# A router's top two found inside the attention stage, two groups at a time, in place of its logits

## The chip, the cores and the metric

One Trainium2 chip, one core. The metric is the device time of one execution in microseconds (us), the median of three runs. Kernel and reference work in float32. TensorE is called PE, VectorE DVE, ScalarE ACT, GpSimd POOL; SP is the engine whose queue issues most DMAs.

## What is computed

The input x has 4 sequences of 2048 tokens with 256 features. Three residual blocks follow each other:

```python
x = x + 0.5 * ffn(layernorm(x))
x = x + attn(layernorm(x))
x = x + 0.5 * ffn(layernorm(x))
```

`ffn` is a mixture of 8 experts. The part that matters here is its router:

```python
logits = xf @ router_w.T                 # 8192 tokens x 8 experts
probs = softmax(logits)
topw, topi = top_k(probs, 2)
topw = topw / (topw.sum(-1) + 1e-6)
# each expert keeps its 1280 tokens of highest weight (ties by token number)
# and adds weight * (silu(x@wg) * (x@wu)) @ wd to them
```

`attn` is a gated delta-rule recurrence over time with 8 heads of 32 features (projections, a chain over time, a gated norm and an output projection), and a small MLP with silu behind it.

## The kernel before

Five stages follow each other on the one core: the first layer norm with the first router logits (`first_norm`), `route` and `experts` for the first mixture, `attention`, and `route` and `experts` for the second. In the profile they take about 0 to 117, 117 to 207, 207 to 1080, 1080 to 2592 and 2592 to 3569 us.

`attention` cuts time into 64 chunks of 32 steps. The 128 partitions hold 4 sequences by 32 steps; four chunks are a group, so there are 16 groups, g = 0 to 15. A group passes five generators: `stage_load`, `stage_proj`, `stage_prep` (decays, and the triangular inverse on DVE in lines 870 to 891), `stage_chain` (the recurrence) and `stage_out` (lines 973 to 1044). `weave` (line 1048) runs the generators of neighbouring groups by turns. Each `yield` gives the PE time, the wait and the DVE work of the step just emitted, and `weave` picks the next step from these numbers and from due times with a period of 78 us. PE keeps exactly the order that `weave` emits. The other engines are ordered by the framework's scheduler when the program is built, by program order and by priorities (`urgent()` and `first()` raise them). On the chip each engine takes its instructions strictly in that order and waits on semaphores.

What `stage_out` does, by line: 976 to 978 scale the sums of squares `sx` and run a Newton reciprocal root (`newton`, lines 643 to 648) into `rx`; 988 makes `hh` on ACT from it, which PE transposes (658); 997 to 1018 are the MLP; 1023 to 1027 the layer norm's statistics; 1031 makes `xn`; 1036 transposes it; 1040 multiplies by the router's weights into `pl`; 1041 copies the 8 logits of each of the 128 tokens of a chunk into the tile `logits2` (128 partitions, 64 chunks by 8 experts); 1043 stores `xn`. Other instructions that the prediction names: `qa` and `gg` (lines 758 to 771, a series for softplus in `stage_prep`, DVE), `gm` (777, POOL, four instructions per group, made from `gg`), `pd` (798, PE, from `gm`), `Z` (923) and `OS` (930), DVE transposes of the recurrence that PE waits for, `O` (938), and the POOL products of lines 816 to 867 and 980.

`top2` (line 169) does the router's softmax and picks the two experts. It has 24 DVE instructions and one ACT Exp, nearly all in one chain: each takes what the one before it made. It is called four times in `first_norm`, for 16 chunks each, and once behind `attention`, for all 64 chunks (line 1155). Its result W lies expert by expert, `[P, E, NCH]`, while the logits and its inner tiles lie chunk by chunk, `[P, NCH, E]`. `route` then copies W to ACT (316), stores it to DRAM and reads it back in another layout (324, 326), and starts a search for each expert's threshold (336 and on); `find` (291) and `place` (463) are constants that it loads on the SP queue.

Of the kernel before, what the change touches and what calls it, by code (L numbers as in the profile page):

```python
# [9 lines left out]
F32 = mybir.dt.float32  # L10
# [3 lines left out]
ALU = mybir.AluOpType  # L14
AX = mybir.AxisListType
# [3 lines left out]
P = 128  # L19
B = 4  # L20
C = 32
GC = 4
# [3 lines left out]
E = 8  # L26
# [61 lines left out]
def bc(ap, axes, shape):  # L88

    for a in axes:  # L90
        ap = ap.unsqueeze(a)
    return ap.to_broadcast(list(shape))
# [3 lines left out]
def macaron_kernel(  # L96
# [5 lines left out]
    nc = tc.nc  # L102
    T = x.shape[1]
    NCH = T // C
# [6 lines left out]
    xf, outf = (a.rearrange("b t d -> (b t) d") for a in (x, out))  # L111
# [13 lines left out]
    with tc.tile_pool(name="cst_b", bufs=1) as bp:  # L125
        brief = bp.tile([P, _W - _KEPT], F32, name="cst_b")
# [34 lines left out]
    def store_group(rows, xt, g):  # L161
        for b in range(B):
            r0 = b * T + g * GC * C
            nc.sync.dma_start(
                out=rows[r0 : r0 + GC * C, :].rearrange("(c t) d -> t c d", t=C),
                in_=xt[b * C : (b + 1) * C, :, :],
            )

    def top2(pool, logits, W):

        n = logits.shape[1]
        TE = [P, n, E]

        def t(shape, name):
            return pool.tile(shape, F32, tag=f"t2_{name}", name=name)

        mx, pr, sm = t([P, n], "mx"), t(TE, "pr"), t([P, n], "sm")
        nc.vector.tensor_reduce(mx, logits, AX.X, ALU.max)
        nc.vector.tensor_tensor(pr, logits, bc(mx, [2], TE), ALU.subtract)
        nc.scalar.activation(pr, pr, AF.Exp)  # L180
        nc.vector.tensor_reduce(sm, pr, AX.X, ALU.add)
        nc.vector.reciprocal(sm, sm)
        nc.vector.tensor_tensor(pr, pr, bc(sm, [2], TE), ALU.mult)

        rev = bc(K["rev8"], [1], TE)
        oh, mk = [], []
        for k in range(2):
            mxk, f, fm, ohk = t([P, n], f"mx{k}"), t(TE, "first"), t([P, n], "fm"), t(TE, f"oh{k}")
            nc.vector.tensor_reduce(mxk, pr, AX.X, ALU.max)
            nc.vector.tensor_tensor(f, pr, bc(mxk, [2], TE), ALU.is_equal)  # L190
            nc.vector.tensor_tensor(f, f, rev, ALU.mult)
            nc.vector.tensor_reduce(fm, f, AX.X, ALU.max)
            nc.vector.tensor_tensor(ohk, rev, bc(fm, [2], TE), ALU.is_equal)
            if k == 0:
                nc.vector.scalar_tensor_tensor(pr, ohk, -2.0, pr, ALU.mult, ALU.add)
            oh.append(ohk)
            mk.append(mxk)
        den = t([P, n], "den")
        nc.vector.tensor_tensor(den, mk[0], mk[1], ALU.add)
        nc.vector.tensor_scalar(den, den, 1e-6, None, ALU.add)  # L200
        nc.vector.reciprocal(den, den)
        for k in range(2):
            nc.vector.scalar_tensor_tensor(mk[k], mk[k], 0.5, den, ALU.mult, ALU.mult)
            nc.vector.tensor_tensor(oh[k], oh[k], bc(mk[k], [2], TE), ALU.mult)
        nc.vector.tensor_tensor(W.rearrange("p e c -> p c e"), oh[0], oh[1], ALU.add)

    def first_norm(brief, W, xn_d):

        MC = 8
        xc, nc_ = (a.rearrange("(p c) d -> p c d", p=P) for a in (xf, xn_d))
        logits = brief.tile([P, NCH, E], F32, name="logits")
        with tc.tile_pool(name="in", bufs=3) as ip, tc.tile_pool(name="in_t", bufs=3, space=PSUM) as tps, tc.tile_pool(
            name="in_l", bufs=2, space=PSUM
        ) as lps:
            some = [MC // 2] * 2
            c0 = 0
            for IC in some + [MC] * ((NCH - 2 * MC) // MC) + some:
                xt = ip.tile([P, MC, D], F32, name="xt_in")[:, :IC, :]  # L220
                nc.sync.dma_start(out=xt, in_=xc[:, c0 : c0 + IC, :])
                st = ip.tile([P, MC, 6], F32, name="in_st")
                mv = ip.tile([P, MC, 2], F32, name="in_mv")[:, :IC, :]
                for c in range(IC):
                    nc.vector.bn_stats(st[:, c, :], xt[:, c, :])
                    nc.vector.bn_aggr(mv[:, c, :], st[:, c, :])
                ve = ip.tile([P, MC], F32, name="in_ve")[:, :IC]
                nc.vector.tensor_scalar(ve, mv[:, :, 1], LN_EPS, None, ALU.add)
                r = ip.tile([P, MC], F32, name="in_r")[:, :IC]
                rsqrt(ip, r, ve, IC, "in")  # L230
                nm = ip.tile([P, MC], F32, name="in_nm")[:, :IC]
                nc.vector.scalar_tensor_tensor(nm, mv[:, :, 0], -1.0, r, ALU.mult, ALU.mult)
                xn = ip.tile([P, MC, D], F32, name="in_xn")[:, :IC, :]
                for c in range(IC):
                    if c % 2:
                        nc.scalar.activation(
                            xn[:, c, :], xt[:, c, :], AF.Identity, scale=r[:, c : c + 1], bias=nm[:, c : c + 1]
                        )
                    else:
                        nc.vector.tensor_scalar(  # L240
                            xn[:, c, :], xt[:, c, :], mv[:, c, 0:1], r[:, c : c + 1], ALU.subtract, ALU.mult
                        )
                nc.sync.dma_start(out=nc_[:, c0 : c0 + IC, :], in_=xn)
                pl = lps.tile([P, MC, E], F32, name="pl_in")[:, :IC, :]
                for c in range(0, IC, 2):
                    tp = tps.tile([P, 2, 2, P], F32, name="tp_in")
                    for i in range(2):
                        for k in range(2):
                            nc.tensor.transpose(tp[:, i, k, :], xn[:, c + i, k * P : (k + 1) * P], ident)
                    xnT = ip.tile([P, 2, 2, P], F32, name="in_xnT")  # L250
                    nc.scalar.copy(xnT, tp)
                    for i in range(2):
                        for k in range(2):
                            nc.tensor.matmul(  # L254
                                pl[:, c + i, :], xnT[:, i, k, :], rw[:, k, :], start=(k == 0), stop=(k == 1)
                            )
                nc.scalar.copy(logits[:, c0 : c0 + IC, :], pl)
                c0 += IC
                if c0 % (2 * MC) == 0:
                    cs = slice(c0 - 2 * MC, c0)  # L260
                    top2(ip, logits[:, cs, :], W[:, :, cs])

    behind = tc.keep_in_program_order

# [309 lines left out]
                    if t0 == 0 and e + 1 < E:  # L574
                        find(e + 1)

    def attention(x1_d, logits, xn_d, x2_d):
        GH = GC * H
        CH = [P, GC, H]
        CHI = [P, GC, H, C]  # L580
# [1 line left out]
        with ExitStack() as st:  # L582
# [3 lines left out]
            wp, p1, p2, p3, p4 = pool("w", 1), pool("1", 1), pool("2", 2), pool("3", 3), pool("4", 4)  # L586
# [386 lines left out]
            def stage_out(g):  # L973
# [9 lines left out]
                for c0 in range(0, GC, 2):  # L983
                    hT2 = p2.tile([P, 2, 2 * P], F32, tag="hT2", name="hT2")
                    for i in range(2):
                        c = c0 + i
# [18 lines left out]
                    for i in range(2):  # L1005
                        c = c0 + i
# [23 lines left out]
                for c in range(GC):  # L1030
                    nc.scalar.activation(
                        xn[:, c, :], xt[:, c, :], AF.Identity, scale=r3[:, c : c + 1], bias=nm3[:, c : c + 1]
                    )
                    yield 0, 0.6
                    xnT = p3.tile([P, 2, P], F32, tag="hT", name="xnT")
                    transposed(xn[:, c, :], xnT)
                    yield 0.25, 0.7
                    pl = tpp.tile([P, E], F32, tag="tp", name="pl")
                    for k in range(2):
                        nc.tensor.matmul(pl, xnT[:, k, :], rw[:, k, :], start=(k == 0), stop=(k == 1))  # L1040
                    nc.scalar.copy(logits[:, g * GC + c, :], pl)
                    yield 0.4, 0.3
                store_group(xn_d, xn, g)
                del live[g]

            plans = {}
# [88 lines left out]
    xn2 = dram.tile([N, D], F32, name="xn2")  # L1135
# [9 lines left out]
                experts(1, wp, ready, place16, *found, xn1, x1_d)  # L1145


    logits2 = keep.tile([P, NCH, E], F32, name="logits2")
    attention(x1_d, logits2, xn2, outf)


    with tc.tile_pool(name="brief2", bufs=1) as brief:
        W = brief.tile([P, E, NCH], F32, name="W2")
        with tc.tile_pool(name="top2", bufs=1) as pool:
            top2(pool, logits2, W)
        with tc.tile_pool(name="ex_w2", bufs=2) as wp, tc.tile_pool(name="place2", bufs=1) as rp:
            ready, place16 = [], places(rp, 2)
            found = route(brief, 2, W, wp, ready, xn2)
            with tc.manual_schedule(engines={mybir.EngineType.PE}):
                experts(2, wp, ready, place16, *found, xn2, outf)  # L1160

# [28 lines left out]
```

## Time and profile before

| what | value |
|---|---|
| runs | 3569.07, 3577.85, 3581.4 us (median 3577.85) |
| profiled execution | 3570.8 us, its span 3569.0 us |
| granted PE clock, mean | 0.96 |
| PE, matmul busy | 3149.7 us, 88% of the span |
| DVE busy | 1665.6 us, 47% |
| ACT busy | 966.8 us, 27% |
| POOL busy | 739.1 us, 21% |
| table loads on ACT (1283 ns each) | 50 |
| last logits copied (line 1041) | begins at 2592.19 us |
| W2 written (line 205) | ends at 2607.41 us |

A line of a time line reads: start, duration, engine, line of the kernel, operation, output from inputs, shapes, count, and in brackets the idle time of that engine just before and what ended it. A busy PE is not PE at its peak, since matmuls are pipelined. The granted clock is 1.0 or 0.5 in each interval; a mean under 1 says for what share of the time PE ran at half rate.

### The profile page before, as it was taken

To read this page: it belongs to the slowest core of one execution; us is meant where nothing else is said; L and a number is where in the kernel's file an instruction comes from. 1 tells how busy PE (TensorE), PEld (TensorE's weight loads), DVE (VectorE), ACT (ScalarE), POOL (GpSimd) and SP (SyncE) were. 2 spreads that over 40 slices of the span, in tenths; PEclk is the share of its full clock that TensorE was granted. 3 is DMA by queue.
4 is the path that set the end of the run, shared out by engine and by line. 5 is a ranking of instruction groups with operands and counts; after the bars stand their busy time and mean duration, and the time that the engine had idled before them with its cause. 6 is when DMAs were issued, how large, how long until landed. Compare 5 with 4: busy or idle time off the path is not lost.

```text
span 3569.0 us, 74202 instructions
## 1 busy us (share of the span) xinstructions
PE 3149.7 (88%) x31911; PEld 2162.5 (61%) x31911; DVE 1665.6 (47%) x4844; ACT 966.8 (27%) x2222; POOL 739.1 (21%) x794
## 2 busy tenths in 40 slices
PE   7279999999995588999999999899817999999998
PEld 6246666666662366666666666667714666666666
DVE  6751222221116747778777777665284122222111
ACT  3212211112213233343443434333221122111121
POOL 0031332222211111112112122111003123222121
PEclk9999999999997799999999999999858999999999
DMA  4512222222112000010110000000021222122211
GB/s 171 198 24 58 64 51 40 60 52 59 30 15 70 2 20 3 20 26 19 26 27 20 20 20 20 14 14 15 19 87 30 54 61 65 27 60 59 54 27 15
DMA packets 94791, 153.10 MB, mean 43 GB/s; under 512 B 13368, under 2 KB 77760, under 8 KB 92800
## 3 DMA queue, kind: packets, MB, share of 16 engines
q1 hardware_dynamic: 63648, 106.15, 9.5%
q0 software_dynamic: 30816, 42.23, 7.4%
q8 instruction: 250, 4.10, 0.5%
q14 instruction: 77, 0.63, 0.1%
HBM read 101.67 MB, written 55.05 MB: 44 GB/s over the span
## 4 chain that ended last, share of the span: by engine, by line
PE 71%; DVE 21%; ACT 3%; issue 2%; DMA 2%; POOL 1%; SPq 0%; POOLq 0%; DVEq 0%; ACTq 0%
PE pg L551 15%; PE po L564 15%; PE pu L553 15%; DVE tm L875 4%; DVE X L879 4%; PE pp L718 3%; PE py L1009 3%; PE pc L635 3%; PE pgk L635 2%; PE pl_in L254 1%; PE ppo L965 1%; DVE over L357 1%; PE tp L658 1%; PE tpx L525 1%; PE pd L798 1%
## 5 line engine op out<-in xcount | busy, mean ns | idle before, releaser
L556 DVE TENSOR_TENSOR hT<-sg,pu 128x512 f32<-128x512 f32 (+1 forms) x384 | 229.3, 597 | 1136.7 <-PE pu L553 1135.5
L551 PE MATMUL pg<-xT,wg_e 128*128 128x512 f32 (+1 forms) x1536 | 617.4, 524 | 0.9 <-ACT xT L526 0.9
L553 PE MATMUL pu<-xT,wu_e 128*128 128x512 f32 (+1 forms) x1536 | 613.4, 522 | 0.0
L564 PE MATMUL po<-wd_e,hT 128*128 128x256 f32 x2560 | 560.4, 379 | 0.0
L564 PEld LDWEIGHTS po<-wd_e,hT 128*128 128x128 f32 x2560 | 485.3, 190 | 73.1 <-issue 8.6
L553 PEld LDWEIGHTS pu<-xT,wu_e 128*128 128x128 f32 x1536 | 292.3, 190 | 259.5 <-issue 243.6
L551 PEld LDWEIGHTS pg<-xT,wg_e 128*128 128x128 f32 x1536 | 280.8, 191 | 204.3 <-issue 191.5
L555 ACT ACTIVATE sg<-pg 128x512 f32<-128x512 f32 (+1 forms) x384 | 201.9, 526 | 688.4 <-PE pg L551 685.5
L1009 PE MATMUL py<-wpj,mT 128*128 128x256 f32 x1024 | 264.2, 393 | 15.6 <-DVE xt L1016 8.7
L519 POOL DMA_INDIRECT xg<-xn,idx x160 | 198.7, 1242 | 366.4 <-PE tpx L525 188.3
L718 PE MATMUL pp<-wk,hT 128*128 128x512 f32 x512 | 269.5, 622 | 5.6 <-ACT hT L660 5.4
L570 POOL DMA_INDIRECT x_d<-eo,idx x80 | 131.0, 1638 | 543.5 <-ACT eo L569 378.2
L570 POOL DMA_INDIRECT out_dram<-eo,idx x80 | 128.9, 1611 | 543.5 <-ACT eo L569 374.1
L1009 PEld LDWEIGHTS py<-wpj,mT 128*128 128x128 f32 x1024 | 185.2, 191 | 74.1 <-DVE xt L1016 17.7
L491 DVE TENSOR_TENSOR oa<-aM,iota 128x2048 bf16<-128x2048 bf16 x64 | 145.5, 2283 | 161.6 <-PE pi L503 161.6
L569 ACT ACTIVATE eo<-po,ws 128x256 f32<-128x256 f32 x160 | 75.8, 473 | 522.2 <-PE po L564 522.2
L980 POOL TENSOR_TENSOR xt<-xt,x 128x256 f32<-128x256 f32 x64 | 48.4, 757 | 720.6 <-DVE x L967 373.3
L875 DVE TENSOR_TENSOR tm<-X 128x30 f32<-128x30 f32 (+14 forms) x480 | 156.2, 325 | 11.1
L879 DVE TENSOR_TENSOR X<-X,tm 128x30 f32<-128x30 f32 (+14 forms) x480 | 155.5, 324 | 10.9
L526 ACT COPY xT<-tpx 128x256 f32<-128x256 f32 x160 | 59.6, 372 | 255.8 <-PE tpx L525 255.8
L718 PEld LDWEIGHTS pp<-wk,hT 128*128 128x128 f32 x512 | 89.7, 195 | 41.8 <-issue 22.8
L635 PE MATMUL pc<-WQD,OS 32*32 32x96 f32 x4032 | 108.2, 246 | 1.5 <-issue 1.5
(744 smaller groups left out, 4006.6 us busy)
## 6 DMA issues: line engine op xcount, KB each, us to landing
wg_e<-in_L_ffn_wg_dram SPq DMA_DIRECT2D x16, 1024.0 KB, 5.2
wu_e<-in_L_ffn_wu_dram SPq DMA_DIRECT2D x16, 1024.0 KB, 6.9
wd_e<-in_L_ffn_wd_dram SPq DMA_DIRECT2D x16, 1024.0 KB, 5.7
xt<-x_d SPq DMA_DIRECT2D x64, 128.0 KB, 3.0
out_dram<-xt SPq DMA_DIRECT2D x64, 128.0 KB, 2.3
xn<-xn SPq DMA_DIRECT2D x64, 128.0 KB, 2.3
xt_in<-in_L_attn_x_dram SPq DMA_DIRECT2D x6, 1024.0 KB, 7.0
xn<-in_xn SPq DMA_DIRECT2D x6, 1024.0 KB, 4.8
```

The costliest lines, as they stand in the source:

```text
L519: nc.gpsimd.indirect_dma_start(out=xg, out_offset=None, in_=xn_d[:], in_offset=bass.IndirectOffsetOnAxis(ap=idx[:, t : t + 1], axis=0),)
L551: nc.tensor.matmul(pg[:, :n], wg_e[:, k, fs], xT[:, k, cols], start=(k == 0), stop=(k == 1))
L553: nc.tensor.matmul(pu[:, :n], wu_e[:, k, fs], xT[:, k, cols], start=(k == 0), stop=(k == 1))
L555: nc.scalar.activation(sg[:, :n], pg[:, :n], AF.Silu)
L556: nc.vector.tensor_tensor(hT[:, f, :n], sg[:, :n], pu[:, :n], ALU.mult)
L564: nc.tensor.matmul(po, hT[:, f, (t - t0) * P : (t - t0 + 1) * P], wd_e[:, f, :], start=(f == 0), stop=(f == FF // P - 1),)
L570: nc.gpsimd.indirect_dma_start(out=acc[:], out_offset=bass.IndirectOffsetOnAxis(ap=idx[:, t : t + 1], axis=0), in_=eo, in_offset=None, com ...
L635: nc.tensor.matmul(out[q], lhsT[q], rhs[q], start=first, stop=True, skip_group_check=True)
L718: nc.tensor.matmul(pp, hT[:, k, :], wk[:, k, j * 2 * D : (j + 1) * 2 * D], start=(k == 0), stop=(k == 1),)
L875: nc.vector.tensor_tensor(tmv, Xm[:, j + 1 :, j : j + 1].to_broadcast([P, n, j]), Xm[:, j : j + 1, :j].to_broadcast([P, n, j]), ALU.mult,)
L879: nc.vector.tensor_tensor(Xm[:, j + 1 :, :j], Xm[:, j + 1 :, :j], tmv, ALU.add)
L1009: nc.tensor.matmul(py, mT[:, f, i * P : (i + 1) * P], wpj[:, f, :], start=(f == 0), stop=(f == FF // P - 1),)
```

## The change

`top2` gets W alone and works in it: the copies out of PSUM put the logits straight into W, and softmax and the two picks run in W through a view that swaps experts and chunks. The separate tile `pr` and the logits tiles go. In `attention` the second router's `top2` is called at the end of `stage_out` of every odd group, for the 8 chunks of that group and the one before, with its small tiles in a pool of `attention` with one buffer. The single call for 64 chunks behind `attention` goes. No `yield` follows the new call, so `weave` counts nothing for it.

```diff
-    def top2(pool, logits, W):
-        n = logits.shape[1]
+    def top2(pool, W):
+        n = W.shape[2]
+        pr = W.rearrange("p e c -> p c e")
...
-        nc.vector.tensor_reduce(mx, logits, AX.X, ALU.max)
-        nc.vector.tensor_tensor(pr, logits, bc(mx, [2], TE), ALU.subtract)
+        nc.vector.tensor_reduce(mx, pr, AX.X, ALU.max)
+        nc.vector.tensor_tensor(pr, pr, bc(mx, [2], TE), ALU.subtract)
...
-        nc.vector.tensor_tensor(W.rearrange("p e c -> p c e"), oh[0], oh[1], ALU.add)
+        nc.vector.tensor_tensor(pr, oh[0], oh[1], ALU.add)
...
     # first_norm
-                nc.scalar.copy(logits[:, c0 : c0 + IC, :], pl)
+                nc.scalar.copy(W[:, :, c0 : c0 + IC].rearrange("p e c -> p c e"), pl)
...
-                    top2(ip, logits[:, cs, :], W[:, :, cs])
+                    top2(ip, W[:, :, cs])
...
     # stage_out of attention
-                    nc.scalar.copy(logits[:, g * GC + c, :], pl)
+                    nc.scalar.copy(W[:, :, g * GC + c], pl)
                     yield 0.4, 0.3
                 store_group(xn_d, xn, g)
+                if g % 2:
+                    top2(p1, W[:, :, (g - 1) * GC : (g + 1) * GC])
                 del live[g]
...
-    logits2 = keep.tile([P, NCH, E], F32, name="logits2")
-    attention(x1_d, logits2, xn2, outf)
+    W2 = keep.tile([P, E, NCH], F32, name="W2")
+    attention(x1_d, W2, xn2, outf)
...
-        W = brief.tile([P, E, NCH], F32, name="W2")
-        with tc.tile_pool(name="top2", bufs=1) as pool:
-            top2(pool, logits2, W)
```

More of the change, by code (lines that the diff above doesn't have):

```diff
@@ L175, in t @@
             return pool.tile(shape, F32, tag=f"t2_{name}", name=name)
-        mx, pr, sm = t([P, n], "mx"), t(TE, "pr"), t([P, n], "sm")
-        nc.vector.tensor_reduce(mx, logits, AX.X, ALU.max)
-        nc.vector.tensor_tensor(pr, logits, bc(mx, [2], TE), ALU.subtract)
+        mx, sm = t([P, n], "mx"), t([P, n], "sm")
+        nc.vector.tensor_reduce(mx, pr, AX.X, ALU.max)
+        nc.vector.tensor_tensor(pr, pr, bc(mx, [2], TE), ALU.subtract)
         nc.scalar.activation(pr, pr, AF.Exp)
@@ L212, in first_norm @@
         xc, nc_ = (a.rearrange("(p c) d -> p c d", p=P) for a in (xf, xn_d))
-        logits = brief.tile([P, NCH, E], F32, name="logits")
         with tc.tile_pool(name="in", bufs=3) as ip, tc.tile_pool(name="in_t", bufs=3, space=PSUM) as tps, tc.tile_pool(
@@ L575, in experts, with attention @@
                         find(e + 1)
-    def attention(x1_d, logits, xn_d, x2_d):
+    def attention(x1_d, W, xn_d, x2_d):
         GH = GC * H
@@ L1145, in macaron_kernel @@
                 experts(1, wp, ready, place16, *found, xn1, x1_d)
-    logits2 = keep.tile([P, NCH, E], F32, name="logits2")
-    attention(x1_d, logits2, xn2, outf)
+    W2 = keep.tile([P, E, NCH], F32, name="W2")
+    attention(x1_d, W2, xn2, outf)
     with tc.tile_pool(name="brief2", bufs=1) as brief:
-        W = brief.tile([P, E, NCH], F32, name="W2")
-        with tc.tile_pool(name="top2", bufs=1) as pool:
-            top2(pool, logits2, W)
         with tc.tile_pool(name="ex_w2", bufs=2) as wp, tc.tile_pool(name="place2", bufs=1) as rp:
             ready, place16 = [], places(rp, 2)
-            found = route(brief, 2, W, wp, ready, xn2)
+            found = route(brief, 2, W2, wp, ready, xn2)
             with tc.manual_schedule(engines={mybir.EngineType.PE}):
```

## The prediction

> **What bounds the kernel now.** I read the busy shares by slice, the time line around the last logits copy, and then, stage by stage, what PE waits for in attention. The granted clock by slice (40 slices of 89 us, tenths of full speed) comes first, and then the window of attention that is in steady state, with the columns window, length, busy PE, PE weight load, DVE, ACT, POOL (instructions behind each), clock, DMA share, GB/s.
>
> ```profile
> PEclk9999999999997799999999999999858999999999
> 1340.00:2500.00 1160.00, 1072.27 (x20441) 770.22 (x20437) 854.17 (x2829) 444.28 (x1099) 227.47 (x381) 0.98 0.08 19
> ```
>
> The reader is to see that PE is busy 92% of the window in which the new calls land, and DVE 74%. PE bounds it and DVE has 306 us to spare; but PE can lose time where it waits for a DVE chain, and DVE works strictly in its built order. The call that goes stands in the 8 in PEclk, between the last logits and route:
>
> ```profile
> 2592.19 0.17 ACT L1041 COPY logits<-pl 128x8 f32<-128x8 f32 x1 [1.11 <-PE pl L1040]
> 2592.37 1.28 ACT L180 ACT_TABLE_LOAD   x1
> 2592.39 0.69 DVE L178 TENSOR_REDUCE mx<-logits 128x64 f32<-128x512 f32 x1 [9.17 <-ACT logits L1041]
> ...
> 2593.83 0.63 ACT L180 ACTIVATE pr<-pr 128x512 f32<-128x512 f32 x1 [0.18 <-DVE pr L179]
> ...
> 2606.39 1.02 DVE L205 TENSOR_TENSOR W<-oh,oh 128x512 f32<-128x512 f32 x1
> 2607.44 0.38 SPq L324 DMA_DIRECT2D wl_d<-W  x1
> ```
>
> From the last copy's end, 2592.36, W takes 15.05 us to 2607.41, then the store follows at once. Nothing else runs on PE: this is on the path.
>
> **Part 1, the tail: less.** A call for 8 chunks works on 64 elements a partition in place of 512. An operation of 512 took 0.69 us, one of 128 (first norm's calls) 0.29; with the 0.03 us between dependent ones that is 0.72 and 0.32, a slope of 1.04 ns an element, so about 0.255 for 64 and 0.20 for the narrow ones. Working in W makes operands strided: line 205, the only strided one of the chain, took 1.02 against 0.69, 0.65 ns an element, or 0.04 at 64. The table load (1.28 us) and the Exp it serves stay. In the built order that load now stands behind the wait for the subtraction, so `sm` begins at about 2594.5 as before; what follows is 21 operations, 4.85 us in place of 12.9. W ends at about 2599.35: **minus 8.0** (7.5 to 8.5). In the built order the W store now also stands ahead of the loads of `find` and `place` on SP's queue. They are hidden by the store's landing (issued 2607.44, the next load 2610.03) and by the WL load behind it, whose reader starts at 2612.72; without that cover they cost 0 to 2.
>
> **Part 2, first norm: more.** Its four calls do nine more strided operations each, of 128 elements: 9 x 128 x 0.65 ns = 0.75 us a call. The last call is on the path surely (it ends the stage, at about 117 us). For the others, DVE has idle time, but PE waits 15.9 us in all for DVE there. I take **plus 2.0**, between 0.3 and 3.6.
>
> **Part 3, seven calls inside attention: more.** The eighth odd group's call is the tail. Each of the seven puts 24 instructions into DVE's order. By work alone it is little: 24 x 0.2 = 5 us a call, 35 of the 306 us that DVE has idle. What matters is what they stand ahead of. In the built order they are interleaved, from the logits copies on, with `qa`, `gg` and the Newton root of the next group; that next group's `hh` on ACT, its transpose on PE and all PE work behind it wait for the root. Between the last logits copy of the odd group and the end of that `rx`, the built order puts 11 top2 instructions (group 1), 23 (3), 11 (5), 8 (7), 11 (9), 24 (11), 2 (13). The place for group 1:
>
> ```profile
> 1449.17 2.43 POOL L777 TENSOR_TENSOR gm<-gg,cst 128x256 f32<-128x256 f32 x4 [2.57 <-DVE nw L646]
> 1449.33 0.47 DVE L648 SCALAR_TENSOR_TENSOR rx<-nw,rx 128x4 f32<-128x4 f32 x1
> ...
> 1449.84 0.91 ACT L988 ACTIVATE hh<-x,rx 128x256 f32<-128x256 f32 x2 [1.32 <-DVE rx L648]
> ...
> 1450.40 0.44 PE L658 MATMUL tp<-cst,hh 128*128 128x128 f32 x2 [1.77 <-ACT hh L988]
> ```
>
> PE already waits 1.77 us here, so every further delay of `rx` is a delay of PE. Also see that `rx`, four elements, took 0.47 beside POOL's `gm`, against 0.15 for the same operation just before. The next place, group 3, shows this with PE's wait of 2.17 us:
>
> ```profile
> 1620.65 2.33 POOL L777 TENSOR_TENSOR gm<-gg,cst 128x256 f32<-128x256 f32 x4 [0.65 <-DVE sx L976]
> ...
> 1621.32 0.54 DVE L646 TENSOR_TENSOR nw<-nw,sx 128x4 f32<-128x4 f32 x1
> ...
> 1622.93 0.30 DVE L923 STREAM_TRANSPOSE Z<-pc 128x128 f32<-128x128 f32 x1
> ...
> 1623.29 1.07 PE L635 MATMUL pc<-KP,Z 32*32 32x64 f32 x32 [2.17 <-DVE nw L646]
> ```
>
> A DVE operation with two inputs (or a scalar on f32) takes one POOL product, 0.58 to 0.61 us, while `gm` runs; transposes, reductions and reciprocals do not. 16 of the 24 new ones are of the blocked kind, 8 free of it.
>
> Group 1: seven top2 operations of about 0.15 us and a transpose of 0.44 now stand ahead of `gg` (before, it ended at 1449.03), less slack that was there: plus 1.2, with a wait for Exp of 0.1 to 0.4 in it. Then more top2 operations go under `gm`'s four products, so `gg` to `rx` is 2.99 us and not 0.77: plus 2.2. Sum 3.4 (2.0 to 4.5); groups 5 and 9 have the same pattern, and the same figure. Group 3: `Z` 0.9 late and `rx` 3.6, 3.6 taken (1.5 to 5). Group 7: eight operations ahead of `gg`, 1.7 late, but the transpose of `hh` there has some 4 us to spare: 1.5 (0 to 3). Group 11: the calls fall into gaps in which DVE waits for line 967's input: 0.2 (0 to 1). Group 13: only here the Exp needs the table changed and back (50 loads become 52, of 1.28 us); one stands ahead of an `hh` with 0.7 to spare: 1.0 (0.5 to 2). Together 10.2 + 3.6 + 1.5 + 0.2 + 1.0 = **plus 16.5** (7.5 to 24).
>
> **Part 4, the clock.** Behind a wait PE is granted half the clock in some places: after the 2.17 us above for 3.4 us (1623.35 to 1626.76), after 2.34 at 1363 for 3.4, after 4.01 at 2463.6 for 6.8, around 5.81 at 2306.88 for 20.5. After 1.77, 1.69, 1.48 and another 2.17 it stayed full. A product of line 965 took 1.13 us warm and 2.08 cold, so a cold stretch costs about half its length where PE bounds. The waits of groups 1, 5 and 9 become about 5.2 us (1.77 + 3.4 and alike), between the 4.01 and the 5.81 row. I go by the 4.01 row, which is nearest to a wait of this form (one chain, then full work): 3.4 a place, less what is slack in the cold stretch, 2.5; group 3 adds 1.7, half of one 3.4 stretch more. 7.5 + 1.7 = **plus 9.2**. Ends: 0 (as after the other 2.17 row) and 33 (three times 10.2 as after the 5.81 row, and 2).
>
> A rule that weighs this otherwise: the Trainium skill, *TensorE: Matmul & The Clock Gate*, "What's actually happening", says that the clock falls after one idle window of some 3.4 us and returns after one busy window. The rows of 3.4 us agree in length; the stretch of 20.5 does not fit one window. By the rule only the three waits of 5.2 cool, a window each: 5.1 in place of 9.2, and the sum 4 less.
>
> **Sum.** 3570.8 (the profiled execution; its span is 3569.0) - 8.0 + 2.0 + 16.5 + 9.2 = 3590.5. The three runs have their median 7 above the profiled execution and one run 2 below it; I take half, so **3594**.
>
> **Rivals.**
> *The cover holds* (0.27): DVE swallows the seven calls in its waits, PE gets `hh` and `Z` on time, and only tail and first norm count. For it: 35 us of work against 306 idle; `hh` has slack in groups 7 and 11. Against it: PE's 1.77 and 2.17, which say that this chain is already the last to come. It decides if the delay of `rx` in groups 1, 3, 5, 9 stays under about 1 us each, or is made up by work of the next rounds that PE does not have to wait for. Price: -8.0 + 2.0 + 0 to 6 = -6 to 0, so 3565 to 3578. Not slower.
> *The clock stays down* (0.13): the 5.2 us waits are followed by 20 us at half clock as at 2306.88, 10 each for 2.5 at three places or more: 3594 + 22 = 3616, between 3612 and 3640. For it the row of 20.5; against it the 4.01 row.
> *The tail is not shortened* (0.05): the loads of `find` and `place` behind the store, or DVE work left over from group 15, hold the search's start; less than 4 of the 8 is saved, and the time is 3598 to 3606.
> The forecast (0.55) has the range 3580 to 3612 of its own.
>
> **How the numbers follow.** About 0.3%, 10.7 us of 3577.85, is what a measurement of this kernel can tell from no change: 3567.1 to 3588.6. Faster by more would need the whole tail, 8.5, and a cold stretch of before that goes: 0.06, out of the first rival. Within: 0.20 of that rival and 0.12 of the forecast, 0.32. Slower: 0.62. The range runs from 3571, inside the first rival, to 3622, inside the second; it leaves out about 0.1 on each side.
>
> **What would show it.** Right: PE waits of about 5 us for `hh` of ACT near 1450, 1796 and 2141, and of some 5 for `Z` and `hh` near 1624; 0.5 in the clock behind them; `rx` under `gm` with top2 operations of 0.54 before it; W ended 7 us after the last logits copy; the first stage 2 us longer; 52 table loads. Wrong: waits of PE there under 3 us (the cover held), new waits at the even groups or in the inverse, which I priced at nothing since there no top2 operation stands between, or a tail over 10 us.

## The result and the profile after

The changed kernel takes 3600.01 us as a median of five runs (3594.52 to 3603.9), against 3577.85 before (3569.07 to 3581.4): a ratio of 1.006 with a 95% interval of 1.0049 to 1.0071. It is slower by 0.6%; 0.45% was forecast. Its profiled execution took 3600.17 us, 29.4 more than that of before, with a span of 3597.0, 28.0 more. The granted clock by slice, and the window of attention with the columns of the prediction's first fence:

```profile
PEclk9999999999997799999999999989858999999999
```

```profile
1340.00:2500.00 1160.00, 1065.34 (x20028) 761.10 (x20028) 870.26 (x2945) 436.07 (x1073) 225.53 (x377) 0.97 0.07 18
```

DVE works 16 us more in the window and PE does 7 less in it. The one slice of attention whose clock falls from 9 to 8 says little: it holds the 20.5 us at half clock that the profile of before has too (from 2302.6 there, from 2335.8 here).

The place behind group 1 in the time line of the changed kernel (start, duration, engine, line, operation, operands, shapes, idle time just before and its cause):

```profile
1456.35 0.15 DVE L771 TENSOR_TENSOR gg<-za,nA 128x32 f32<-128x32 f32 x1
...
1456.64 2.62 POOL L777 TENSOR_TENSOR gm<-gg,cst 128x256 f32<-128x256 f32 x4 [3.83 <-DVE first L192]
1456.82 0.21 DVE L193 TENSOR_REDUCE fm<-first 128x8 f32<-128x64 f32 x1
1456.95 0.45 DVE L646 TENSOR_TENSOR nw<-nw,sx 128x4 f32<-128x4 f32 x1
1457.32 0.21 DVE L194 TENSOR_TENSOR oh<-cst,fm 128x64 f32<-128x64 f32 x1
1457.46 0.57 DVE L647 SCALAR_TENSOR_TENSOR nw<-nw 128x4 f32<-128x4 f32 x1
1457.95 0.26 DVE L196 SCALAR_TENSOR_TENSOR W<-oh,W 128x64 f32<-128x64 f32 x1
1458.12 0.58 DVE L648 SCALAR_TENSOR_TENSOR rx<-nw,rx 128x4 f32<-128x4 f32 x1
...
1459.30 0.69 PE L658 MATMUL tp<-cst,hh 128*128 128x128 f32 x2 [4.46 <-ACT hh L988]
```

Lines 192 to 196 of `top2` now stand between the steps of the Newton root (645 to 648), and the last three of those steps (646 to 648) take 0.45 to 0.58 us beside POOL's `gm`. `rx` begins 1.77 us behind the start of `gg` where it began 0.49 behind it before, and PE waits 4.46 us for `hh` in place of 1.77. The two PE transposes that follow already take 0.69 in place of 0.44: the clock is down. The waits of PE in attention, in the columns waited for, total, times, longest, first before (1433 to 2593 us), then changed (1440 to 2620):

```profile
PE tp L658 <- ACT hh L988: 8.8, 7, 1.8
PE pW L635 <- DVE XT L890: 8.2, 4, 4.0
```

```profile
PE tp L658 <- ACT hh L988: 20.7, 8, 4.5
...
PE pW L635 <- DVE XT L890: 8.3, 4, 4.0
```

`hh` has 11.9 us more; the inverse's result XT, which no call stands ahead of, is unchanged. Behind groups 1, 5 and 9 the granted clock is 0.5 for 10.2 us each (from 1458.6, 1813.6 and 2168.6), where before it did not fall. Behind group 1, before and then changed, in the columns of the prediction's first fence:

```profile
1449.70:1459.90 10.20, 9.50 (x186) 6.06 (x186) 7.79 (x23) 7.92 (x18) 8.63 (x16) 1.00 0.01 2
1458.60:1468.80 10.20, 9.51 (x72) 4.63 (x76) 7.07 (x31) 4.19 (x11) 5.43 (x11) 0.50 0.00 0
```

PE is as busy as before, but gets through 72 matmul instructions in place of 186. Measured by the last logits copy of each group, the changed kernel falls behind like this:

| stretch | lost, us | at half clock, before and after |
|---|---|---|
| first norm (W1 written at 117.11 and 120.19) | 3.1 | |
| from there to group 1 | 3.1 | |
| group 1 to 2, 5 to 6, 9 to 10 | 7.16, 6.94, 6.83 | 0 and 10.2 each |
| group 3 to 4 | 2.49 | 3.4 and 3.4 |
| group 6 to 7 (no call stands in it) | 3.25 | 0 and 6.8 |
| all other stretches from group 1 to 15 together (the calls of groups 7, 11 and 13 stand in them) | 0.04 | |
| last logits copy to the search's start | -5.7 | |
| the search and the second experts | 0.8 | |

The tail of the changed kernel in its time line:

```profile
2625.11 0.17 ACT L1041 COPY W<-pl 128x8 f32<-128x8 f32 x1 [1.11 <-PE pl L1040]
...
2631.91 0.27 DVE L206 TENSOR_TENSOR W<-oh,oh 128x64 f32<-128x64 f32 x1
...
2632.24 0.39 SPq L324 DMA_DIRECT2D wl_d<-W  x1
...
2632.86 0.39 SPq L463 DMA_DIRECT2D place<-in_consts_dram  x1
2633.34 0.46 SPq L291 DMA_DIRECT2D find<-in_consts_dram  x1
...
2633.56 1.03 POOL L310 DMA_INDIRECT row<-xn,row  x1 [0.15 <-DVE tl L337]
...
2634.95 0.33 SPq L326 DMA_DIRECT2D WL<-wl_d  x1
...
2639.91 0.43 DVE L335 TENSOR_SCALAR WS<-WL 128x512 int32<-128x512 int32 x1 [3.46 <-DMA WL<-wl_d]
```

W is written 6.9 us behind the copy's end, not 15.05. But from the issue of WL to its reader 4.96 us pass; before it was 2.69 (2610.03 to 2612.72). So 2.3 of the 8.2 us gained are given back.

### The profile page after: what moved, and what is told of

It reads as the page before. It is cut to its first block, busy times and chain, and to the rows that moved or that the text cites. A ratio compares the mean times of both kernels' runs of the same rounds, so it can differ in the third digit from the quotient of the medians.

```text
span 3597.0 us, 74375 instructions
## 1 busy us (share of the span) xinstructions
PE 3168.8 (88%) x31911; PEld 2172.3 (60%) x31911; DVE 1687.3 (47%) x5012; ACT 973.1 (27%) x2231; POOL 742.9 (21%) x794
## 4 chain that ended last, share of the span: by engine, by line
PE 70%; DVE 21%; ACT 3%; DMA 2%; issue 2%; POOL 1%; SPq 0%; POOLq 0%; DVEq 0%; ACTq 0%
PE pg L551 15%; PE pu L553 15%; PE po L564 15%; PE pp L718 4%; DVE tm L875 4%; DVE X L879 3%; PE py L1009 3%; PE pc L635 3%; PE pgk L635 2%; DVE over L357 1%; PE tp L658 1%; PE ppo L965 1%; PE pl_in L254 1%; PE pd L798 1%; PE tpx L525 1%
```

## The experiments

Theory: the seven calls cost because of their place in DVE's order, ahead of the chain `gg`, `rx`, `hh` that PE already waits for, and the wait pulls the clock down. Rivals: the strided layout, the sum of DVE work, and the later start of attention. Ratios are to before, timed beside it on the same chip; in brackets is the 95% interval.

**e1, the layout alone.**

```diff
-                if g % 2:
-                    top2(p1, W[:, :, (g - 1) * GC : (g + 1) * GC])
...
     attention(x1_d, W2, xn2, outf)
+    with tc.tile_pool(name="top2", bufs=1) as pool:
+        top2(pool, W2)
```

> The layout alone: logits go straight into W, first norm's calls work in W, and the second router's call stays one call of 64 chunks behind attention, in W. Theory (the seven calls cost, because they stand ahead of rx and gg): first norm ends 3.1 us later as in the changed kernel (119.81 against 116.73 for W's last instruction), attention has none of its 27 us, the 64-chunk call takes 15.05 + 9 x 0.33 = 18.0 us; in all about +6 over before, 3581 to 3587 as a median. It also shows whether the 3.4 us that the changed kernel loses between 1162 and 1342 us, ahead of its first call, come with the later start alone. Rival (the strided layout itself costs in attention, by ACT's copies into W and W's rows): attention longer by 10 or more, 3594 or more.

Measured: 3587.87, ratio 1.0025 (1.0016 to 1.0034); just above the range expected. Attention loses nothing from group 1 to 15 (4.20 us behind, then 3.23), so the rival of the layout falls. The 64-chunk call took 19.78 us, 4.7 more and not 3: its table load now stands behind the subtraction, where before it ran beside it (1.28 us), and its Exp in W took 1.06 us in place of 0.63. First norm missed the expectation: W's last instruction began at 115.37, not 119.81, though the code is that of the changed kernel (more on this below).

**e2, first norm as before.**

```diff
-                nc.scalar.copy(W[:, :, c0 : c0 + IC].rearrange("p e c -> p c e"), pl)
+                nc.scalar.copy(logits[:, c0 : c0 + IC, :], pl)
...
-                    top2(ip, W[:, :, cs])
+                    top2_apart(ip, logits[:, cs, :], W[:, :, cs])
```

> The changed kernel with first norm as before (its own logits tile, contiguous, W written once by the last operation); the seven calls and the tail as changed. Theory: 3.1 us less at W's last instruction of first norm, attention's 27 us unchanged, 3600 - 3 = 3597, or 3593 if the 3.4 us ahead of the first call go with it. Rival (a later start moves attention against the chip's clock windows and that made much of the loss): 3585 or less.

Measured: 3596.56, ratio 1.0046 (1.0032 to 1.006). The interval overlaps that of the changed kernel, so the medians don't settle first norm's price; but the loss at the three places is the same (7.03, 7.02, 6.93), so the start of attention did not make it. At the second of them half clock lasted 6.8 us and not 10.2, and the loss is 7.02 all the same.

**e3, the same calls behind the next group's rx.**

```diff
-    def top2(pool, W):
+    def top2(pool, W, late=None):
...
+        if late is not None:
+            nc.vector.tensor_copy(mx[:, 0:1], late)
         nc.vector.tensor_reduce(mx, pr, AX.X, ALU.max)
...
                 newton(p2, rx, sx, GC, "x")
+                if g and g % 2 == 0:
+                    top2(p1, W[:, :, (g - 2) * GC : g * GC], rx[:, 0:1])
...
-                if g % 2:
+                if g == NG - 1:
                     top2(p1, W[:, :, (g - 1) * GC : (g + 1) * GC])
```

> The changed kernel with each of the seven calls emitted in the next group's stage_out, behind its Newton root, and bound to it: one more DVE operation per call writes a column of rx into mx, which the maximum then overwrites. So rx stands ahead of all 24 instructions; their number and kind stay. Theory (the place in DVE's order is what costs, with the clock behind it): PE's waits for hh at the even groups fall back from 4.5 to about 1.8 us, the 10.2 us stretches at half clock go; 7 x 3 + 3 x 2 = 24 to 27 less, against 0 to 6 new (the rest of the call now stands ahead of gg's successors and the start of the inverse): 3573 to 3582. Rival (24 more instructions of DVE cost wherever they stand, or POOL's gm beside them): 3592 or more.

Measured: 3580.97, ratio 1.0006 (0.9994 to 1.0017): as before, 19 us less than the changed kernel, with one DVE instruction more per call. The place behind group 1 in e3's time line:

```profile
1459.43 2.43 POOL L779 TENSOR_TENSOR gm<-gg,cst 128x256 f32<-128x256 f32 x4 [2.57 <-DVE nw L648]
1459.59 0.47 DVE L650 SCALAR_TENSOR_TENSOR rx<-nw,rx 128x4 f32<-128x4 f32 x1
...
1460.66 0.44 PE L660 MATMUL tp<-cst,hh 128*128 128x128 f32 x2 [1.42 <-ACT hh L992]
1460.68 0.26 DVE L181 TENSOR_REDUCE mx<-W 128x8 f32<-128x64 f32 x1
```

`rx` starts under the first of `gm`'s four products as it did before, and the call's first reduction comes when PE already transposes `hh`. Groups 1, 5 and 9 lose 0.39, 0.19 and 0.15 us. The place is shown as the cause of what these three lose. The moved calls are not free, though: from group 1 to 15 this profile falls 7.8 us behind that of before, where the changed kernel falls 26.7 behind and e1, with no call in attention, none. The other profiles in which all seven calls are moved say the same (e5 8.3, e6 8.6, e7 9.1, e10 8.4). So the rival of the work's sum falls for some 19 of the 27 us; the rest stays wherever the calls stood. In all of them 2.55 to 2.94 us go between groups 2 and 3, with at least 6.8 us at half clock where before has none, though PE's waits just ahead are no longer than before (1.2 us for `xn`); why is open.

**e4, PE kept busy through the wait.** The ten products are extra work whose result is not used.

```diff
                         yield 0, 0.6
+                        if c == 0 and g in (2, 6, 10):
+                            pf = tpp.tile([P, 2, P], F32, tag="tp", name="pf")
+                            for _ in range(10):
+                                nc.tensor.matmul(pf.rearrange("p a c -> p (a c)"), ident, wf[:, 0, : 2 * P], start=True, stop=True)
                         transposed(hh, hT2[:, :, i * P : (i + 1) * P])
```

> The changed kernel with ten products of 128x128 by 128x256 on PE (3.9 us at full clock by the 0.39 us of such a row), read by nobody, in PE's order just ahead of the first transpose of hh in groups 2, 6 and 10, where PE waits 4.5 us. They fill the wait and delay nothing if the wait is real. Theory (about half of the 7 us at each place is the half clock behind the wait): the stretches of 10.2 us at half clock go, each 3 to 4 us less: 3588 to 3592. Rival (the loss is the wait alone): 3600, or up to 3 more where the products outlast the wait.

Measured: 3600.25, ratio 1.0056 (1.0042 to 1.007): nothing gained, against my theory. The profile says what happened, here behind group 5:

```profile
1812.74 4.58 PE L993 MATMUL pf<-wf,cst 128*128 128x256 f32 x20
...
1817.29 0.44 PE L658 MATMUL tp<-cst,hh 128*128 128x128 f32 x2
...
1823.00 0.45 PE L635 MATMUL pc<-XT,vg 32*32 32x32 f32 x32 [0.70 <-DVE OS L930]
...
1828.78 1.13 PE L1001 MATMUL pm__15746<-hT,wf 128*128 128x256 f32 x4 [1.53 <-ACT mT L1007]
```

The products fill the wait and the transposes keep 0.44; at groups 5 and 9 no half clock follows. Yet 5.03 us are lost at both, 1.9 and 1.8 less than in the changed kernel. With PE at full speed two waits show that before did not have here, 0.70 and 1.53 us: for `OS`, which DVE reaches late behind the call's rest and the statistics that it pushed back, and for ACT's `mT`, likely late through it. So of the 7 us at such a place some 2.8 are the longer wait for `hh`, some 2.2 are this further lateness, and only 1.9 the half clock. In other places stretches at half clock were added (10.2 us from 1540, and 6.68 us lost between groups 1 and 2), and the sum stayed.

**e8, only the calls of groups 1, 5 and 9 moved.** The edit is that of e3 with `if g in (2, 6, 10):` at the root and `if g % 2 and g not in (1, 5, 9):` at the end of the group.

> The changed kernel with only the calls of groups 1, 5 and 9 moved behind the next group's rx, as in e3; those of 3, 7, 11 and 13 stay at the end of their groups. Theory (by the changed kernel's shift against before, these three places carry 6.9 to 7.2 us each, groups 3 and 7 2.5 and 3.3, the others nothing): 20 of the 27 us in attention go, 3582 to 3587, and the shift stays flat at the three places. Rival (the loss follows the sum of the work, each call alike): 3600 less three sevenths of 24, about 3590 or more.

Measured: 3586.16, ratio 1.0018 (1.0003 to 1.0032): as the theory has it. Its profile is of one of its longest executions, 3600.47. In it 0.41 and 0.18 us are lost behind groups 1 and 5; behind 9, though, 3.23, with 6.8 us at half clock, and 6.13 between groups 3 and 4, with 10.2 us of it.

**e7, the calls later, in the inverse.** The edit is that of e3 with the call in the MLP's loop, `if c0 == 0 and g and g % 2 == 0:`, bound to `mv[:, 0, 0:1]`.

> The seven calls later still: bound to the first layer norm statistics that the next group's MLP makes, so that they fall into the triangular inverse (lines 870 to 891 of the kernel before), a chain on DVE alone. There each call's Exp needs ACT's table changed twice: 12 loads of 1.28 us more. Theory (what counts is what PE waits for behind the place): the inverse becomes up to 6 us longer in seven groups, and PE waited for its result XT in four places only, up to 4 us; so 1 to 4 us per group and the Exp's loads in the way of ACT's Silu, 3588 to 3610. Rival (every place off the rx chain is covered by DVE's idle time): 3578 to 3584, as e3.

Measured: 3585.39, ratio 1.0015 (1.0003 to 1.0026). Both expectations missed it, mine by more. PE's waits in e7 from 1440 to 2620 us:

```profile
PE pW L637 <- DVE XT L892: 9.3, 4, 4.0
```

XT costs PE one us more and not up to 28: the inverse had cover, which I had not measured. Even where PE already waited for XT behind a call (1.92 and 1.73 us before), the wait grew by 0.5 only. So not every place ahead of a DVE chain is dear, and a wait of PE behind it does not settle how dear it is. The intervals of e7 and e3 overlap.

**e5 and e9, what held WL.** e5 is e3 with `behind(...)` (keep in program order) around the loads of `place` and `find` and W's store.

> e3 (calls behind the next group's rx) with one more change: the loads of place and find are kept ahead of the store of W on SP's queue, as they stood in the kernel before. In e3 and in the changed kernel they are issued behind the store, and from the issue of WL's load to its first reader 5.3 and 5.0 us pass, before it was 2.7. Theory (the two loads, now on the way at the same time, hold WL): 2.7 again, the stretch from W's last instruction to that reader 5.3 us, all in all 2.5 less than e3. Rival (WL is held by the expert weights issued behind it or by POOL's row gather, which now comes at the same time): still about 5. The median differs by less than the runs scatter; the profile decides.

Measured: 3581.11, ratio 1.0004 (0.999 to 1.0017); WL's issue to its reader 5.3 us, so this theory fell. `place` and `find` went out only at 2613.07 and 2613.53, behind W's end (2612.94) and 0.9 and 0.5 us ahead of the store (2614.00), not the 0.05 that e9's expectation names. e9 is the changed kernel with e5's order and this:

```diff
-                if g % 2:
+                if g % 2 and g < NG - 1:
...
     attention(x1_d, W2, xn2, outf)
+    with tc.tile_pool(name="top2", bufs=1) as pool:
+        top2(pool, W2[:, :, NCH - 2 * GC :])
...
-            nc.vector.memset(row0, 0)
+            nc.gpsimd.memset(row0, 0)
```

> The changed kernel with the last group's call behind attention, with tiles of its own pool, as the one call of before had; place and find ahead of W's store; and the memset of the row index (line 308) on POOL in place of DVE. The seven calls inside attention stay as changed. Reason: e5 had place and find ahead of the store, and they were still issued only when W was done, 0.05 us ahead of the store, as the memory of attention's pools comes free only with the last call; and POOL's row gather (line 310) came 1.1 us behind W, where before it came 6 us ahead. Theory (what holds WL is the traffic that the late release of that memory brings beside it: row gather, place, find): place, find and the gather go out within 3 us of the last logits copy, WL's issue to its first reader 2.7 us as before in place of 5.0, the stretch from W's last instruction to that reader 5.3 in place of 7.7. Rival (the expert weights behind WL hold it, coming sooner against something else): still about 5. The rest of the time as the changed kernel, 3594 to 3604 less 2.4.

Measured: one run, 3598.35. Its tail:

```profile
2625.18 0.35 SPq L463 DMA_DIRECT2D place<-in_consts_dram  x1
...
2626.62 1.06 POOL L310 DMA_INDIRECT row<-xn,row  x1
...
2633.18 0.38 SPq L324 DMA_DIRECT2D wl_d<-W  x1
...
2635.77 0.33 SPq L326 DMA_DIRECT2D WL<-wl_d  x1
...
2638.43 0.43 DVE L335 TENSOR_SCALAR WS<-WL 128x512 int32<-128x512 int32 x1 [1.91 <-DMA WL<-wl_d]
```

The transfers go out within 0.6 us of the last copy's end or ahead of it, and WL takes 2.66 us again; from last logits to search 12.2 us, against 14.6 changed and 20.4 before. What held WL was traffic beside it, late most likely since the last call's tiles lay in attention's pool. Of that traffic it was most likely the gather: in e5 `place` and `find` had landed (1.9 and 2.3 us after their issue) when WL was issued, while the gather, issued at 2614.32 and 5.9 us on its way, went beside it. The three were not tried apart with the memory free.

**e6 and e10, a better version.** e6 joins e3, e2 and e5's order, and puts ahead of the last group's `xn` an Exp of one column, so that the table is loaded early:

```diff
+                if g == NG - 1:
+                    nc.scalar.activation(ve[:, 0:1], mv[:, 0, 0:1], AF.Exp)
                 xn = p1.tile([P, GC, D], F32, tag="xn", name="xn")
```

> A version put together from what the runs say: calls behind rx as in e3, place and find ahead of W's store as in e5, first norm with its own contiguous logits as in e2, and a one-column Exp on ACT ahead of the last group's xn, so that the table load of the last call comes while PE still works. Theory: against e3 2.5 less by the loads, 2.7 by first norm, 1.3 by the table; 3573 to 3576, that is 0.9965 to 0.9995 of before. Rival (small waits in attention that go to half clock by chance of the start eat it up): 1.000 to 1.002.

Measured: 3575.23, ratio 0.9989 (0.9977 to 1.0001). W came 5.62 us behind the last logits, 1.3 less, as expected. e10 adds the tail of e9:

> e6 (calls behind rx, first norm as before, early table load) with the tail of e9. If e9's theory holds, 1.3 to 2.5 less than e6: 3572.5 to 3574 or a ratio of 0.9965 to 0.9995. If the memory is not what delays the transfers, as e6: 0.998 to 1.000. The median's scatter is wider than that step; the profile's stretch from the last logits copy to the first reader of WL decides, 20.4 us before, 13.8 in e6, 11 to 12 expected.

Measured: 3575.77, ratio 0.9988 (0.9979 to 0.9997); the tail is 10.9 us, just under what was expected, 9.5 less than before. e10 beats both kernels, before by a tenth of a per cent; that its tail is 2.8 us shorter than e6's does not show in the medians. Its 9.5 us of tail are mostly lost again: from group 1 to 15 it falls 8.4 us further behind, chiefly at groups 1 and 2 (5.8 us), with half clock that before did not have.

## Why the prediction was right

*The forecast*, 3594 with slower at 0.62, held: 3600.01 lies in the range. The sum of its steps is 19.7 us; the medians differ by 22.2, the two profiled spans by 28.0. For groups 1 to 15 it had 16.5 + 9.2 = 25.7 us; 26.7 were measured, which is nearer than its steps deserve, since their errors cancel. By its steps:

*The stall of groups 1, 5 and 9.* The mechanism was right, as e3 shows. Its size was 2.7 us (4.46 less 1.77) at group 1 and 2.95 (4.17 less 1.22) at group 5, where 3.4 was forecast: `gg` came 1.3 late, as worked out (1.2). From its end to the end of `rx` 2.2 us passed, not the 2.99 forecast, so the root under `gm` lost 1.4 and not 2.2. The step that one DVE operation with two inputs takes one POOL product holds for the root's steps at group 3 before (0.46 to 0.54 us each, each made from the one ahead of it), but not here: 646, 194, 647, 196 and 648 passed in 1.75 us, less than three products of `gm` (0.65 us each), and the two of `top2` among them took 0.21 and 0.26 us, where the prediction looked for 0.54.

*The clock.* Half clock came at these three places, but for 10.2 us, where I took the 6.8 of the 4.01 row and 2.5 us of price. The loss less the growth of the wait is 4.0 to 4.5 a place, but e4 shows that the clock alone was worth 1.9 of it. The rest, 2.2, is lateness behind `rx` that the sum had at nothing: the call's other half, which pushes back the next DVE work. So that 5.9 were forecast a place and 6.8 to 7.2 measured is in part luck. The rule of the Trainium skill, *TensorE: Matmul & The Clock Gate*, "What's actually happening", warm again after one busy window of about 3.4 us, would have had the price lower still. Here PE was 93% busy through the stretch (9.51 of 10.2 us behind group 1) and yet three such lengths passed before full clock was granted again; in e2 it was two at one place. Still, by e4's 1.9 a place the price of the clock at the three places is 5.7, nearer to the 5.1 that the prediction worked out by the rule than to its own 7.5.

*The other groups.* Group 3 cost 2.5 and not 3.6 + 1.7: PE's waits there grew from 2.17 to 1.36 + 3.35 us, and the half clock of 3.4 us was there before already. Group 7's call cost 0.2 and not 1.5. The 3.25 us between groups 6 and 7 lie ahead of it, where no call stands: there 6.8 us of half clock follow a wait of 1.77 us for `hh` that was 1.48 before. The prediction had nothing for this, and in e3 and e5, whose waits there are 1.50 and 1.77, nothing is lost. Group 11 cost nothing, as forecast; behind group 13 1.7 went, against 1.0, and the stretches on either side of it gave that back.

*First norm.* 3.1 us against 2.0, of which 0.4 stands in the first copy already (19.1 and 18.7), ahead of any call; so about 0.7 for each of the four calls, nearly all of it on the path. I had counted the last one in full and the rest in part. From the first copy to W, e3, e4, e8 and e9 need what the changed kernel does (101.0 to 101.1 us, against 98.45 before), but e1 and e7, with the same code, only 96.6, and e2 and e6, with the code of before, 95.4. In e1 at least, PE ran faster for a while (the same four transposes take 0.64 us at 57.57 there and 1.09 at 56.93 before). Like against like, the layout costs some 1.2 to 2.6 us here.

*The tail.* W came 8.2 us earlier, forecast 8.0. What failed is the step that WL's load keeps its 2.7 us and so is a cover for the loads of `find` and `place`: it was itself held, 2.3 us. In e9, with place, find and gather gone out ahead of it, this is gone; in e5, with the two loads landed and the gather still on its way, it is not. The gather is not in the prediction. The third rival named the loads, but at a price that left less than 4 of the 8; 5.7 were left.

*What the sum lacked.* Between first norm and group 1 another 3.1 us went, with no call there. In all eleven other profiles of this study that stretch is 3.1 to 10.8 us longer than in the profile of before, e1 among them. So the profile of before is of a lucky execution there (its 3570.8 is 7 below its kernel's median), and these 3.1 us are hardly a price of the change. That it is the clock, below, is likely and was not tried.

*The rivals.* The cover did not hold: PE's waits were the sign, as the prediction argued against it. Still e7 shows that cover exists elsewhere, and group 7 had it. The 20 us of half clock did not come.

## What to carry to other kernels

Before work is put on an engine with idle time, look in the built order at which chain it will stand ahead of, and whether PE already waits for that chain's end: there every us by which the end comes later counts fully. Here 2.8 us more of waiting became 7, by half clock and by what the call pushed back further. The same instructions a few places later cost some 8 us in attention in place of 27, and with the shorter tail the whole kernel took as long as before (e3: 0.9994 to 1.0017). And work that keeps a pool alive longer can also delay the transfers into the memory that follows, as the tail suggests.

## What the runs showed of the hardware

The stretches of half clock begin on a grid. The longest of the profile before, 122.88 us, is 36 times 3.4133 us, and the other stretches, but for the one cut off by the end, are whole multiples of that too. Taken modulo this length, all 14 of that profile begin at 2.01, all 20 of the changed one at 1.09; e3's at 0.94, e5's at 2.45. The grid does not follow the kernel. That the window is free-running is what the Trainium skill says in the place named above, and these rows agree. e3 and e5 have the same attention; behind group 1 PE waited 1.42 us in e3 and lost 0.39, and waited 1.75 in e5 and lost 3.23, with 6.8 us at half clock. Waits of the same length fare differently too: 1.77 us for `hh` was followed by no half clock before (at 1450.40) and by 6.8 us of it in the changed kernel (at 1904.35); 4.0 us for XT by 6.8 us before (at 2463.61) and by 3.4 in the changed kernel (at 2496.29). So what such a wait costs depends on where it falls. Those of 4.2 to 4.5 were followed by three lengths of half clock at each of the three places in the changed kernel and in e9, and at two of the three in e2, by two lengths at the other. This is a likely reason for the scatter of the runs (e8's reach from 3576 to 3602 us); it was argued from these profiles, not tried by itself.

The recorded clock of a profile's first part has to be read with care: for the four transposes of first norm named above the record gives 1.00 in both profiles, though they take 1.09 us in one and 0.64 in the other.
